# A sparse two-layer graph network on one core: ScalarE takes part of the list sorting, and the order around it changes

## The chip, the cores and the metric

The kernel runs on one core of a Trainium2 chip. The metric is the device time of one execution in microseconds; the median of three runs of the kernel before is 1572.41 us (1570.78 to 1575.34). Five engines work side by side, each through its own instructions in order: TensorE (PE; its weight loads are listed as PEld), VectorE (DVE), ScalarE (ACT), GpSimd (POOL) and SyncE (SP, which here only issues DMA transfers).

## What is computed

There are 16 graphs of 1024 nodes with 64 channels, and a dense weighted adjacency of 16 x 1024 x 1024, of which few entries are not zero. Two layers follow each other, each on the normed input and with a residual:

```
# layer 0: mean over the neighbours
h = relu(layernorm(x));  x = x + (adj / clip(adj.sum(2), 1)) @ h

# layer 1: per node a weighted quantile over its neighbours, then a small MLP
h = relu(layernorm(x))
nb = (adj > 0) without the diagonal;  m = nb.sum(-1)
skip = (m+1)//2 if m > 10 else 1               # every skip-th neighbour of a long list is removed,
removed = ...;  rem = removed | removed.T      # in both directions
vals = h[neighbours and self, not rem], sorted per channel
agg = 0.25*q(0.25) + 0.5*q(0.5) + 0.25*q(0.75) # each q interpolates between two sorted values
y = relu((h + agg) @ W1 + b1) @ W2 + b2;  x = x + y * mask
```

## The kernel before

**Layer 0.** The adjacency is read once, 128 rows at a time (tile `at`). ACT takes the sign of each row and its sum, DVE finds the numbers of the neighbours in it with Max8 (`listing`), PE turns it, and PE multiplies (`products`). `endings` sorts the nodes of a graph by the length of their list and scatters their records (channels, residual, list, number, mask) into a DRAM table `srt`, so that nodes of like length lie together. Four graphs make a group; there are four groups. `progress["batches"]` counts the graphs that are done.

**Lists.** `group(g)` reads the records of a group (`recs`, rows of 136 bytes), gathers one adjacency row for each node of the tile with the longest lists (`gat_rows`), works out from that which two neighbours are dropped and writes it into the DRAM table `tab`. It extracts the neighbours' numbers and makes jobs of them, one for each length class: ten in a group, for lists of 15 down to 1 places, with T nodes in each partition. `long_lists` does the like for the nodes with the longest lists, in four jobs of up to 88, 31, 24 and 20 places over all groups. There DVE searches the row for its numbers in many rounds of Max8 and MatchReplace (`lfound`, `lkeys`).

**A job** (`Job.run`, `sort`, `layers`): POOL gathers one place for each list entry by indirect DMA (64 channels and two numbers for each of 128 partitions) into A, named `places` or, for a long list, `lplaces`. DVE compares the two numbers with its own node number (`rem`, `gone`), counts what is valid and starts the weights (`wu`, finished by two ACT instructions). One wide DVE instruction adds 1e30 to the dropped places. Then DVE runs a sorting network of min and max instructions between A and a second copy (`other` in PSUM, or `long_other` in SBUF). The sorted places are multiplied by their weights, into `prod` for a short job and in place for a long one; `copies` says in which of the two copies (0 is A) each sorted place ended. PE adds the products up through the identity matrix (`pt`), ACT copies the sum out (`ot`), PE and ACT run the MLP (`ph`, `hid`, `py`, the first and last in `ps_small` banks). DVE adds the residual (`y`), and POOL scatters the finished rows to the output.

**The order.** The order of DVE and POOL instructions is written out in full by a planner at build time (`Plan`, lines 218 to 321). All parts are streams: a `yield` names an engine and a function that says when the next step can start. The planner keeps a clock for each engine, books a duration for each instruction (`note`), and always takes the stream that can start first; between equals the lower rank goes first. The durations are only a model: for ACT 0.06 us, 0.86 ns an element and 0.11 for each operand that is a pointer. `at(tile)` is when the tile is ready by the model, `room(name, n)` when a buffer of n comes free. Slack is added where the model must not be trusted: SLACK is 2 us, LOOSE 7. `later` puts the sorting of a job far back unless fewer than AHEAD = 16 gathers are open. On the chip nothing is reordered: if an instruction waits, all behind it on its engine wait.

Of the kernel before, what the change touches and what calls it, by code (L numbers as in the profile page):

```python
# [9 lines left out]
F32 = mybir.dt.float32  # L10
BF = mybir.dt.bfloat16
# [4 lines left out]
OP = mybir.AluOpType  # L16
# [195 lines left out]
AHEAD = 16  # L212
SLACK = 2.0
LOOSE = 7.0


class Timed:
# [13 lines left out]
class Plan:  # L231
# [24 lines left out]
    def room(self, name, bufs):  # L256

        tiles = self.slots.get(name, ())
        if len(tiles) < bufs:
            return 0.0  # L260
        old = tiles[-bufs]
        return INF if self.users[old] else max(self.used.get(old, 0.0), self.ready.get(old, 0.0))

    def at(self, *tiles):
        return max(self.ready.get(t.tensor.name, INF) for t in tiles)

    def note(self, engine, op, args, kwargs):
        if self.own is not None:
            self.clock[engine] = max(self.clock[engine], self.own)
        out = kwargs["out"] if "out" in kwargs else args[0]  # L270
        rest = [*args[0 if "out" in kwargs else 1:], *(v for k, v in kwargs.items() if k != "out")]
        rest = [getattr(v, "ap", v) if type(v).__name__.startswith("Indirect") else v for v in rest]
        rest = [v for v in rest if isinstance(v, bass.AP)]
        size = max(math.prod(v.shape[1:]) for v in (out, *rest[:2]))
        start = max(
            self.clock[engine],
            *(self.ready.get(v.tensor.name, 0.0) for v in rest if self.own is None),
            self.used.get(out.tensor.name, 0.0) if self.own is None else 0.0,
        )
        after = 0.15  # L280
        if engine == "DVE":
            half = op == "tensor_tensor" and all(v.dtype == HF for v in (out, *rest))
            time = 0.04 if op == "memset" else 0.07 + size * (0.57e-3 if half else 1.04e-3)
        elif engine == "ACT":
            pointers = sum(isinstance(kwargs.get(k), bass.AP) for k in ("bias", "scale"))
            time = 0.06 + size * 0.86e-3 + 0.11 * pointers + 0.09 * ("accum_out" in kwargs)
        elif engine == "PE":
            time = 0.1 + math.prod(out.shape[1:]) * 0.88e-3
            if op == "matmul" and rest[0].dtype == F32:
                time *= 2  # L290
        elif engine == "POOL":
            time, after = (1.27, 2.2) if op == "indirect_dma_start" else (0.15, 0.1)
            self.last = None
        else:
            start = max(start, self.clock["DMA"])
            time, after = 0.05, 2.2 + math.prod(out.shape) * 4 / 165e3
            self.clock["DMA"] = start + after - 2.2
        self.clock[engine] = end = start + time
        self.ready[out.tensor.name] = end + after
        for v in rest:  # L300
            self.used[v.tensor.name] = max(self.used.get(v.tensor.name, 0.0), end + after)
        if "accum_out" in kwargs:
            self.ready[kwargs["accum_out"].tensor.name] = end + after
        return start
# [59 lines left out]
def list_path(ctx, tc, x, adj, nodemask, w1, b1, w2, b2, out, go):  # L364
# [434 lines left out]
    class Job:  # L799
# [8 lines left out]
        def run(self):  # L808
            n, T, pool, short = self.n, self.T, self.pool, self.short

            since = []
            own = () if short else (lambda rank: self.rank,)
            pace = lambda: since[0] + 1.3 * len(since) if not short else 0.0
            yield "POOL", lambda: max(
                at(self.idx), room(self.name, self.bufs), room("S", 4) if short else 0.0
            ), *own
            A = self.A = new(pool, [P, n, T, W], F32, self.name, self.bufs, users=1)
            progress["ahead"] += T * (n - 1)
            if short:
                mine = self.S  # L820
                self.S = new(pool, [P, T, C], F32, "S", 4, users=1)
                nc.sync.dma_start(self.S, mine[:, :, :C])
                self.residual = mine[:, :, X1:R0]
            for t in range(T):
                for k in range(n - 1):
                    if t or k:
                        yield "POOL", pace, *own
                    since.append(since[0] if since else plan.clock["POOL"])
                    gather(A[:, k + 1, t, :], self.table, self.idx[:, t, k:k + 1])
                    progress["ahead"] -= 1  # L830
            yield "DVE", lambda: max(
                at(A, self.S) + SLACK, room("prod", 2) if short else 0.0,
                room("other" if short else "long_other", 1),
            ), self.later
            yield from self.sort()

        def later(self, rank):

            return rank - 900 if progress["ahead"] < AHEAD else rank + 2000

        def urgent(self):
            return -1000 if progress["ahead"] < AHEAD else 5000

        def sort(self):
# [5 lines left out]
                rem, A[:, 1:, :, C:],  # L850
                self.node.unsqueeze(1).unsqueeze(3).to_broadcast([P, n - 1, T, 2]), OP.is_equal,
            )
            gone = new(pool, [P, n - 1, T], F32, name + "gone", bufs)
            nc.vector.tensor_tensor(gone, rem[:, :, :, 0], rem[:, :, :, 1], OP.max)
            ok = new(pool, [P, n - 1, T], F32, name + "ok", bufs)
            nc.vector.scalar_tensor_tensor(
# [10 lines left out]
                q, taus.unsqueeze(2).to_broadcast([P, K, T]),  # L867
                valid.unsqueeze(1).to_broadcast([P, K, T]), OP.mult,
            )
            u = new(pool, [P, K, count, T], F32, name + "wu", 1)  # L870
            nc.vector.tensor_tensor(
                u, col_f[:, :count].unsqueeze(1).unsqueeze(3).to_broadcast([P, K, count, T]),
                q.unsqueeze(2).to_broadcast([P, K, count, T]), OP.subtract,
            )
            vals = A[:, 1:, :, :].rearrange("p k t w -> p (k t) w")[:, :, :C]
            nc.vector.scalar_tensor_tensor(
                vals,
                gone.rearrange("p k t -> p (k t)").unsqueeze(2).to_broadcast([P, (n - 1) * T, C]),
                HUGE, vals, op0=OP.mult, op1=OP.add,
            )  # L880
            if short:
                Bt = new(ps_o, [P, 3 * HALF], F32, "other", 1, users=1)
                other = Bt[:, :n * T * C].rearrange("p (k t c) -> p k t c", k=n, t=T)
            else:
                other = Bt = new(pool, [P, n, T, C], F32, "long_other", 1, users=1)
            yield "ACT", lambda: at(u) + SLACK
            nc.scalar.activation(u, u, AF.Abs)
            nc.scalar.activation(u, u, AF.Relu, bias=wt0, scale=-QUANTILES[0][1])

            def places(copy, run, shift=0):  # L890
                first, d1, n1, d2, n2 = run
# [36 lines left out]
            w = new(pool, [P, count, T], F32, name + "w", bufs)  # L928
            nc.vector.tensor_tensor(w, u[:, 0, :, :], u[:, 1, :, :], OP.add)
            nc.vector.scalar_tensor_tensor(w, u[:, 2, :, :], 2.0, w, op0=OP.mult, op1=OP.add)  # L930

            total = max(count + 1, 4)
            prod = None
            if short:
                prod = new(pool, [P, T, total, C], F32, "prod", 2, users=1)
                if count + 1 < total:
                    nc.vector.memset(prod[:, :, count + 1:, :], 0.0)
            for copy in range(2):
                for run in runs_of([k for k in range(count) if copies[k] == copy]):
                    first, step, number = run[:3]  # L940
                    sl = slice(first, first + step * (number - 1) + 1, step)
                    src = places(copy, run)
                    nc.vector.tensor_tensor(
                        prod[:, :, sl, :].rearrange("p t k c -> p k t c") if short else src, src,
                        w[:, sl, :].unsqueeze(3).to_broadcast([P, number, T, C]), OP.mult,
                    )
            if short:
                free(A)
                free(Bt)
                yield "ACT", lambda: at(S)  # L950
                nc.scalar.copy(prod[:, :, count, :], S[:, :, :C])
                free(S)

# [11 lines left out]
        def layers(self, terms, sources):  # L965

            T, R = self.T, terms[0][0].shape[1]
            yield "PE", lambda: max(at(*sources) + LOOSE, room("y", 5), room("pt", 2))
            y = new(mlp, [P, T, CO], F32, "y", 5, users=1)
            x1 = y  # L970
            if self.short:
                nc.sync.dma_start(x1, self.residual)
# [2 lines left out]
            for t0 in range(0, T, 4):  # L975
# [32 lines left out]
                for i, t in enumerate(ts):  # L1008
# [1 line left out]
                        pv[:, i, :], hid[:, i * P:(i + 1) * P], w2_sb, start=False,  # L1010
                        stop=(i == len(ts) - 1),
                    )
                yield "DVE", lambda: at(py) + LOOSE
                for i, t in enumerate(ts):
                    nc.vector.scalar_tensor_tensor(
                        y[:, t, :], pv[:, i, :], self.mask[:, t:t + 1], x1[:, t, :],
# [2 lines left out]
                free(py)  # L1019

            for t in range(T):
                yield "POOL", lambda: at(y) + LOOSE
                scatter(out_rows, y[:, t, :], self.nodes_i[:, t:t + 1], scatters)
            free(y)
            progress["jobs"][self.g] += 1
# [1 line left out]
    def group(g):  # L1027
# [17 lines left out]
        )  # L1045
        nodes_i = new(grp, [P, NTAU], I32, "nodes_i", 2)
        nc.vector.tensor_copy(nodes_i, nodes)
        yield "POOL", lambda: at(nodes_i)
        full = new(grp, [P, N], F32, "gat_rows", 1)
        gather(full, adj_rows, nodes_i[:, 0:1])  # L1050
        yield "DVE", always

        found = new(grp, [P, NTAU, 8 * NSEG], BF, "gfound", 1)
        nc.vector.tensor_scalar(found, lists, 0.0, None, op0=OP.is_gt)
        m = tiny.tile([P, NTAU], F32, name="gm")
        nc.vector.tensor_reduce(m, found, AX.X, OP.add)
# [52 lines left out]
        nc.vector.scalar_tensor_tensor(  # L1109
            full, col_f, node[:, 0:1], full, op0=OP.not_equal, op1=OP.mult  # L1110
        )
        nb = new(grp, [P, N], BF, "nb", 1)
        nc.vector.tensor_scalar(nb, full, 0.0, None, op0=OP.is_gt)
        cum = full
        nc.vector.tensor_tensor_scan(cum, nb, zeros, 0.0, op0=OP.add, op1=OP.add)
# [29 lines left out]
    def long_lists(pool):  # L1145
# [4 lines left out]
        for l, K in enumerate(LONG):  # L1150
# [7 lines left out]
                )  # L1158
            node = S[:, 0, RW - 2:RW - 1]
            mask = S[:, 0, RW - 1:RW]  # L1160
            yield "DVE", lambda: at(S)
            nodes = tiny.tile([P, 1], F32, name="lnodes")
            nc.vector.tensor_tensor(nodes, node, noff[:, 1:2], OP.add)
            nodes_i = new(pool, [P, 1], I32, "lnodes_i", 4)
# [62 lines left out]
            )  # L1227
            plan.add(job.run(), 100 * NG + l)

    progress = {"batches": 0, "groups": 0, "ahead": 0, "jobs": [0] * (NG + 1)}  # L1230
    for g in range(NG):
        plan.add(group(g), -2000)
    with tc.tile_pool(name="lay0", bufs=2) as pool:
# [303 lines left out]
```

## Time and profile before

| stretch, us | DVE busy | ACT busy | POOL busy | PE busy | granted clock |
|---|---|---|---|---|---|
| 0 to 845 (layer 0, first two groups) | 690.6 | 533.5 | 481.4 | 553.6 | 0.79 |
| 845 to 1572 (the rest of the lists) | 569.8 | 45.0 | 507.9 | 190.8 | 0.56 |

The span of the profiled execution is 1571.9 us, with 14933 instructions. DVE is busy for 1260.4 us of it, POOL for 989.3, PE for 744.4 and ACT for 578.5. In the second stretch POOL issues 399 gathers and 71 scatters of output rows.

How to read it: busy time is the union of an engine's instructions; the time from the end of one to the start of the next is idle time, put down to what released the next one ("issue" where nothing was waited for). A line of a group gives the engine, the operation, the names out<-in, how often, the busy time in us, the mean length of one in ns, and behind the second bar the idle time before them. All instructions have the line of the recording helper, L225, so groups are told apart by their tile names. A line of waits gives the sum in us, the number of times and the longest. In a timeline the first numbers are the start and the length in us.

### The profile page before, as it was taken

Reading aid. Unit: us, or ns where it says so; the run is one execution under the profiler, and the core shown is the slowest. Engines: PE = TensorE matmul, PEld = TensorE weight load, DVE = VectorE, ACT = ScalarE, POOL = GpSimd, SP = SyncE. Lnnn points to the kernel's source line nnn. Section 1 sums busy time; section 2 is a strip of 40 time slices with the busy share of each in tenths; the row PEclk is TensorE's granted clock in tenths of the full one; section 3 lists DMA queues with packets and bytes.
Section 4 is the critical chain, followed back from the end, with each engine's and each line's share of the span. In section 5 each row is a group of like instructions: output and inputs, shape, how many; then the busy total and the mean of one; then the engine's idle time right before and its main releaser. Section 6 shows DMA issues by size and latency. Waiting matters only on the chain. (4 is left out here: it accounts for less than half of the span.)

```text
span 1571.9 us, 14933 instructions
## 1 busy us (share of the span) xinstructions
PE 744.4 (47%) x3192; PEld 465.3 (30%) x3192; DVE 1260.4 (80%) x4174; ACT 578.5 (37%) x1746; POOL 989.3 (63%) x1149
## 2 busy tenths in 40 slices
PE   5787776365756754855880001200021367124355
PEld 2334443133343532532450001100021156023244
DVE  6767899997997699999556897659779889878962
ACT  7889888346565536664630000000000010000001
POOL 0222238665578767568676666587777678566775
PEclk8888998686977866976895555555555567555657
DMA  5455666244542433652222111111121111111110
GB/s 161 134 149 167 175 198 188 71 124 100 177 121 60 120 106 108 165 149 66 75 51 66 41 38 36 33 27 23 25 41 34 24 28 24 28 31 36 31 29 21
DMA packets 135530, 128.95 MB, mean 82 GB/s; under 512 B 100696, under 2 KB 103384, under 8 KB 135432
## 3 DMA queue, kind: packets, MB, share of 16 engines
q1 hardware_dynamic: 102696, 86.46, 19.7%
q0 software_dynamic: 32736, 41.47, 11.6%
q8 instruction: 27, 0.44, 0.1%
q14 instruction: 71, 0.58, 0.1%
HBM read 108.57 MB, written 19.28 MB: 81 GB/s over the span
## 5 line engine op out<-in xcount | busy, mean ns | idle before, releaser
L225 POOL DMA_INDIRECT places<-tab,idx x496 | 507.4, 1023 | 159.9 <-issue 146.1
L225 PE MATMUL pt<-ident,prod 128*128 128x128 f32 (+1 forms) x736 | 168.0, 395 | 627.5 <-DVE prod L225 586.7
L225 PEld LDWEIGHTS pt<-ident,prod 128*128 128x128 f32 (+1 forms) x736 | 136.6, 273 | 659.6 <-DVE prod L225 406.0
L225 PE MATMUL ps_small<-att,h 128*65 128x512 f32 x512 | 260.1, 657 | 44.1 <-ACT h L225 28.3
L225 POOL DMA_INDIRECT srt<-row,to x128 | 129.5, 1012 | 176.2 <-ACT row L225 154.8
L225 POOL DMA_INDIRECT lplaces<-tab,lidx x163 | 173.7, 1066 | 51.0 <-issue 47.9
L225 PE MATMUL pt<-ident,at 128*128 128x128 f32 x1024 | 167.3, 308 | 80.7 <-ACT att L225 68.9
L225 POOL DMA_INDIRECT out_dram<-y,nodes_i x124 | 130.6, 1053 | 99.2 <-DVE y L225 53.6
L225 DVE MAX8 rec<-sg 128x8 f16<-128x256 f16 x512 | 180.1, 414 | 4.4
L225 PEld LDWEIGHTS pt<-ident,at 128*128 128x128 f32 x1024 | 129.4, 157 | 126.2 <-ACT att L225 93.7
L225 ACT ACTIVATE sg<-at 128x1024 f16<-128x1024 f32 x128 | 134.9, 1054 | 54.2 <-DMA at<-in_adj_dram 34.6
L225 ACT COPY att<-pt 128x512 f32<-128x512 f32 x256 | 141.5, 582 | 22.7 <-PE pt L225 20.7
L225 ACT COPY ot<-pt 128x128 f32<-128x128 f32 (+3 forms) x56 | 22.2, 401 | 308.9 <-PE pt L225 308.6
L225 ACT ACTIVATE wu<-wu 128x39 f32<-128x39 f32 (+9 forms) x40 | 9.4, 235 | 337.7 <-DVE wu L225 337.6
L225 PEld LDWEIGHTS ps_small<-att,h 128*65 128x65 f32 x512 | 75.8, 154 | 184.3 <-issue 128.5
L225 DVE TENSOR_TENSOR sg<-sg,keyed 128x1024 f16<-128x1024 f16 x128 | 87.6, 684 | 37.3 <-ACT sg L225 37.2
L225 DVE SCALAR_TENSOR_TENSOR y<-ps_small,recs,y 128x64 f32<-128x64 f32 x124 | 28.0, 276 | 81.0 <-PE ps_small L225 80.9
L225 DVE TENSOR_TENSOR other<-places,other 128x64 f32<-128x64 f32 (+6 forms) x204 | 69.7, 342 | 5.6
L225 DVE TENSOR_TENSOR places<-places,other 128x64 f32<-128x64 f32 (+2 forms) x208 | 62.4, 309 | 4.9
L225 DVE TENSOR_TENSOR long_other<-lplaces 128x512 f32<-128x512 f32 (+5 forms) x124 | 63.9, 553 | 0.4
L225 DVE TENSOR_TENSOR lplaces<-long_other 128x512 f32<-128x512 f32 (+7 forms) x116 | 61.4, 567 | 0.1
L225 DVE TENSOR_TENSOR places<-other,places 128x128 f32<-128x128 f32 (+5 forms) x160 | 54.9, 343 | 3.5
(206 smaller groups left out, 1516.1 us busy)
## 6 DMA issues: line engine op xcount, KB each, us to landing
at<-in_adj_dram SPq DMA_DIRECT2D x128, 512.0 KB
places<-tab,idx POOLq DMA_INDIRECT x496
tab<-row SPq DMA_DIRECT2D x16, 264.0 KB
xt<-in_x_dram SPq DMA_DIRECT2D x16, 256.0 KB
lplaces<-tab,lidx POOLq DMA_INDIRECT x163
recs<-srt SPq DMA_DIRECT2D x4, 544.0 KB
srt<-row,to POOLq DMA_INDIRECT x128
out_dram<-y,nodes_i POOLq DMA_INDIRECT x124
```

The source lines that it names most:

```text
L225: ins = getattr(self._engine, op)(*args, **kwargs)
```

## The change

After layer 0 is done (`helped`), ACT takes two parts of the sorting from DVE: the 1e30 for dropped places, one Identity with a bias for each place and node, and the multiplication with the weights, one scaled copy for each: of copy 0 for short jobs and of all places for long ones. The preparation of a job becomes a step of its own before the sort (`soon`), so that ACT can work in between; `gone` and `wu` get buffers for two short jobs. Besides, the search of long lists waits until the last group's records have been begun (`begun`); DMA loads of rows under 512 bytes are booked at a lower rate; the last addition and the scatter of a job are put later in the order (LATE instead of LOOSE); there are six `y` buffers, and two row tiles of a group (`gfound`, `nb`) share one buffer.

```diff
+LATE = 14.0
...
-            time, after = 0.05, 2.2 + math.prod(out.shape) * 4 / 165e3
+            rate = 165e3 if 4 * out.shape[-1] >= 512 else 85e3
+            time, after = 0.05, 2.2 + math.prod(out.shape) * 4 / rate
...
             yield "DVE", lambda: max(
-                at(A, self.S) + SLACK, room("prod", 2) if short else 0.0,
-                room("other" if short else "long_other", 1),
-            ), self.later
+                at(A, self.S) + SLACK,
+                *(room(("" if short else "l") + name, 2 if short else 1) for name in ("gone", "wu")),
+            ), self.soon
             yield from self.sort()
...
+        def soon(self, rank):
+
+            return rank - (950 if progress["ahead"] < AHEAD else -1900)
...
-            gone = new(pool, [P, n - 1, T], F32, name + "gone", bufs)
+            gone = new(pool, [P, n - 1, T], F32, name + "gone", bufs, users=1)
...
-            u = new(pool, [P, K, count, T], F32, name + "wu", 1)
+            u = new(pool, [P, K, count, T], F32, name + "wu", bufs, users=1)
...
-            vals = A[:, 1:, :, :].rearrange("p k t w -> p (k t) w")[:, :, :C]
-            nc.vector.scalar_tensor_tensor(
-                vals,
-                gone.rearrange("p k t -> p (k t)").unsqueeze(2).to_broadcast([P, (n - 1) * T, C]),
-                HUGE, vals, op0=OP.mult, op1=OP.add,
-            )
+
+            helped = progress["batches"] == B
+            if helped:
+                yield "ACT", lambda: at(gone) + SLACK
+                nc.scalar.mul(gone, gone, HUGE)
+                for t in range(T):
+                    for k in range(1, n):
+                        if (t or k > 1) and k % 4 == 1:
+                            yield "ACT", always
+                        val = A[:, k, t, :C]
+                        nc.scalar.activation(val, val, AF.Identity, bias=gone[:, k - 1, t:t + 1])
+            else:
+                vals = A[:, 1:, :, :].rearrange("p k t w -> p (k t) w")[:, :, :C]
+                nc.vector.scalar_tensor_tensor(
...
+            free(gone)
+            yield "ACT", lambda: at(u) + SLACK
+            nc.scalar.activation(u, u, AF.Abs)
+            nc.scalar.activation(u, u, AF.Relu, bias=wt0, scale=-QUANTILES[0][1])
+            yield "DVE", lambda: max(
+                at(A) + SLACK if helped else 0.0, room("prod", 2) if short else 0.0,
+                room("other" if short else "long_other", 1),
+            ), self.later
...
-            yield "ACT", lambda: at(u) + SLACK
-            nc.scalar.activation(u, u, AF.Abs)
-            nc.scalar.activation(u, u, AF.Relu, bias=wt0, scale=-QUANTILES[0][1])
...
+            free(u)
...
-            for copy in range(2):
-                for run in runs_of([k for k in range(count) if copies[k] == copy]):
+
+            helped = progress["batches"] == B
+            for copy in (1, 0):
+                mine = [k for k in range(count) if copies[k] == copy]
+                if helped and (copy == 0 or not short):
+                    yield "ACT", lambda: at(w) + SLACK
+                    for e, k in enumerate(mine):
+                        if e and e % 4 == 0:
+                            yield "ACT", always
+                        for t in range(T):
+                            src = places(copy, (k, 1, 1, 1, 1))[:, 0, t, :]
+                            nc.scalar.activation(
+                                prod[:, t, k, :] if short else src, src, AF.Copy,
+                                scale=w[:, k, t:t + 1],
+                            )
+                    continue
+                for run in runs_of(mine):
...
-                yield "ACT", lambda: at(S)
+                if not helped:
+                    yield "ACT", lambda: at(S)
...
-            yield "PE", lambda: max(at(*sources) + LOOSE, room("y", 5), room("pt", 2))
-            y = new(mlp, [P, T, CO], F32, "y", 5, users=1)
+            yield "PE", lambda: max(at(*sources) + LOOSE, room("y", 6), room("pt", 2))
+            y = new(mlp, [P, T, CO], F32, "y", 6, users=1)
...
-                yield "DVE", lambda: at(py) + LOOSE
+                yield "DVE", lambda: at(py) + LATE
...
-                yield "POOL", lambda: at(y) + LOOSE
+                yield "POOL", lambda: at(y) + LATE
...
         nc.vector.tensor_copy(nodes_i, nodes)
+        progress["begun"] = g + 1
...
-        found = new(grp, [P, NTAU, 8 * NSEG], BF, "gfound", 1)
+        found = new(grp, [P, N], BF, "gfound", 1).rearrange("p (t e) -> p t e", t=NTAU)
...
-        nb = new(grp, [P, N], BF, "nb", 1)
+        nb = new(grp, [P, N], BF, "gfound", 1)
...
-            yield "DVE", lambda: at(S)
+            yield "DVE", lambda: at(S) + SLACK if progress["begun"] == NG else INF
...
-    progress = {"batches": 0, "groups": 0, "ahead": 0, "jobs": [0] * (NG + 1)}
+    progress = {"batches": 0, "begun": 0, "groups": 0, "ahead": 0, "jobs": [0] * (NG + 1)}
```

More of the change, by code (lines that the diff above doesn't have):

```diff
@@ L874, in sort @@
             )
-            vals = A[:, 1:, :, :].rearrange("p k t w -> p (k t) w")[:, :, :C]
-            nc.vector.scalar_tensor_tensor(
-                vals,
-                gone.rearrange("p k t -> p (k t)").unsqueeze(2).to_broadcast([P, (n - 1) * T, C]),
-                HUGE, vals, op0=OP.mult, op1=OP.add,
-            )
+            helped = progress["batches"] == B
[11 more added lines that the diff above has]
+                nc.vector.scalar_tensor_tensor(
+                    vals,
+                    gone.rearrange("p k t -> p (k t)").unsqueeze(2).to_broadcast(
+                        [P, (n - 1) * T, C]
+                    ),
+                    HUGE, vals, op0=OP.mult, op1=OP.add,
+                )
[7 more added lines that the diff above has]
+            ), self.later
             if short:
@@ L937, in sort @@
                     nc.vector.memset(prod[:, :, count + 1:, :], 0.0)
-            for copy in range(2):
-                for run in runs_of([k for k in range(count) if copies[k] == copy]):
+            helped = progress["batches"] == B
[11 more added lines that the diff above has]
+                                scale=w[:, k, t:t + 1],
+                            )
+                    continue
+                for run in runs_of(mine):
                     first, step, number = run[:3]
```

## The prediction

> **What bounds the kernel now.** I read first the share of each engine by stretches, then the costliest groups and the waits after layer 0, then the timelines around single waits. By stretch (columns: PE, PEld, DVE, ACT, POOL busy us, then the granted clock, DMA share, GB/s):
> ```profile
> 0.00:845.00 845.00, 553.55 (x2308) 316.07 (x2308) 690.58 (x2333) 533.54 (x1619) 481.43 (x621) 0.79 0.46 126
> 845.00:1572.00 727.00, 190.84 (x884) 149.23 (x884) 569.82 (x1842) 44.98 (x127) 507.92 (x529) 0.56 0.15 30
> ```
> Two stages. Layer 0 and the first lists end at about 845 us; there VectorE (DVE) is busy 82% and ScalarE (ACT) 63%. In the last 727 us ACT is nearly free (45 us), so work given to it there has room. DVE (570) and GpSimd (POOL, 508) share the load. POOL's number understates it: between two indirect DMAs lies an issue gap of 0.30.
> ```profile
> L225 POOL DMA_INDIRECT places<-tab,idx x236 | 245.2, 1039 | 74.0 <-issue 70.5 <-DMA places<-tab,idx 2.1 <-DMA tab<-drop,didx 1.4
> L225 POOL DMA_INDIRECT lplaces<-tab,lidx x163 | 173.7, 1066 | 51.0 <-issue 47.9 <-PE pt L225 1.6 <-DMA lplaces<-tab,lidx 1.5
> L225 POOL DMA_INDIRECT out_dram<-y,nodes_i x67 | 72.3, 1080 | 57.5 <-DVE y L225 41.1 <-issue 7.3 <-DVE lrem L225 5.4
> ```
> An undisturbed gather starts every 1.25 us (median 0.947 busy + 0.30). POOL runs from 850 to 1564, 714 us. I went through its timeline and added all idle time above 0.3: 72 us. So POOL has about 642 us of work that nothing hides, of which some 49 is stretching: gathers over 0.96 us. DVE has 570 us of work and 120 us of waits. POOL is the tighter engine and the order of both is fixed in the program, so each makes the other wait. The waits:
> ```profile
> DVE y L225 <- PE ps_small L225: 74.1, 16, 9.4
> DVE lrem L225 <- DMA lplaces<-tab,lidx: 21.7, 1, 21.7
> DVE rem L225 <- DMA places<-tab,idx: 14.0, 1, 14.0
> POOL out_dram L225 <- DVE y L225: 41.1, 11, 10.8
> POOL gat_rows L225 <- DVE lkeys L225: 9.9, 1, 9.9
> ```
> DVE reaches the last addition of a job (y) 4.6 us too early on average, since TensorE (PE), at half clock here, has not finished; POOL's scatter then waits behind it. The other DVE waits, lrem and rem, are for gathers: the sign that POOL limits. How a wide DVE instruction stretches a gather (start, length):
> ```profile
> 1041.13 6.02 DVE L225 SCALAR_TENSOR_TENSOR lplaces<-lgone,lplaces 128x5632 f32<-128x5632 f32 x1
> 1041.24 0.37 ACT L225 ACTIVATE lwu<-lwu 128x201 f32<-128x201 f32 x1 [24.68 <-DVE lwu L225]
> 1041.65 0.47 ACT L225 ACTIVATE lwu<-lwu,wt 128x201 f32<-128x201 f32 x1
> 1041.84 6.12 POOL L225 DMA_INDIRECT lplaces<-tab,lidx  x1 [0.30 <-issue]
> ```
> The gather that meets the marking of dropped places takes 6.12 instead of 0.95. A scatter beside the product of 4.56 us at 1299.4 takes 4.47.
>
> **What the Trainium skill says.** (1) "ScalarE: Activation LUTs", section "What ACT_TABLE_LOAD costs": an ACTIVATE with a per-partition pointer as bias takes about 280 ns + 0.833 per element, a second pointer about 93 more, and back-to-back ones overlap by about 93. For 64 elements: 333 alone, 240 in a row. The trace agrees: the squares of layer 0 (one pointer, 64 elements) take 333, and eight Relus with two pointers take 2.76 us together, 0.33 each. (2) "SBUF — State Buffer", section "Who interferes with whom": a DVE instruction with two SBUF inputs holds a port against GpSimd's reads, and it infers that descriptor generation is not hit by it. On this second point the trace differs, by the 6.12 above; I go by the trace. (3) "Perfetto Trace Analysis", section "GPSIMD Engine Instruction": GpSimd spans are unreliable, the spacing of starts is to be used; hence the 1.25 and the waits from the timeline above.
>
> **The change, part by part.**
> *Dropped places to ACT.* After layer 0, 20 short jobs and 4 long ones are sorted. DVE's marking leaves: from the groups by shape 19.6 us short (2 each of 1.50, 1.35, 1.22, 1.15, 1.09, 0.95, 0.82, 0.68, 0.55, 0.48) and 11.5 long (6.0+2.2+1.8+1.5). ACT gets one 64-wide Identity per gathered place: 2x124 + 163 = 411, at 0.24 (page 1) 99 us.
> *Weights to ACT.* The products of copy 0 of short jobs leave DVE, 10.9 us, and all of the long ones, 9.7: lplaces 8.9 and long_other 0.7. ACT gets 122 + 127 = 249 scaled copies, 60 us. Its load becomes 45+160 = 205 of 727: hidden. DVE keeps about 570-52 = 518.
> *What ACT now holds up.* DVE's sorting waits for the marks. For the 88 places of the longest list that is 21 us (6.0 before), for a short job 1.2 to 4.8 (0.5 to 1.5 before). The planner books 0.06+0.055+0.11 = 0.225 for one, near the 0.24, and puts other DVE work between; at 5% to 7% off, 88 of them are 1.3 us late, inside the 2 us slack. Behind ACT's in-order queue stand also the copies that wait for PE (ot, hid). A late PE now delays marks, and so DVE. Bounds: nothing, or for all 24 jobs what DVE waits per y today, 4.6 each, 110 us. I take 25 us of new DVE waits, as the ot copies are planned with slack of their own, and DVE has 120 us of idle time to lose first.
> *POOL freed from wide DVE work.* The two large pieces stretch POOL by 5.2 and 3.5. The remaining 52-10.6 = 41 us of removed DVE work I charge at the mean rate of the other DVE instructions on two SBUF inputs (about 40 us of stretch over 254 long network + 41): 0.14, 6 us. Together 15. Bounds: 9 and 25.
> *LATE and six y buffers.* The addition and the scatter come 7 us later each in the two orders. All DVE y waits but one (9.42) are under 7 us, and the scatters have 14 us: of POOL's 41 (and the 5.4 and 5.4 behind lrem and other) I let 10 stay. Gain on POOL about 35 to 40; I take 30, as some are replaced by other waits, bounds 10 and 42. The sixth y pays for the longer holding; a ps_small bank is held 7 us longer, which matters only in layer 0.
> *Key search after the last group.* Today the search of the longest list (838 to 865) and the beginning of the last group interleave, and POOL waits 9.9 for the group's row number. The search now comes after it. The last group begins when the jobs of the second are done, which LATE puts up to 14 us later in the order; but POOL has some 110 gathers of the third group left, and DVE idles about 20 us around 816 to 838, in which a job of that group can be prepared. The long gathers may start 10 to 20 us later (897.9 now): POOL does short ones meanwhile. I take 7 of the 9.9 as gain; bounds -8 and +10.
> *Packet times, soon, shared gfound, order of copies.* Loads with rows under 512 B are booked at 85 instead of 165 KB per us. The records need 8.6 us from issue to first use (186.2 to 194.8): booked 5.6 before, 8.8 now. Better order, no work of its own: 0. Preparing a job before its sort spends no more DVE time, and gfound is read long before nb is written: 0. Layer 0 loses no DVE work; its order moves, which I bound at +-8 and take at 0.
> Sum: 15+30+7 = 52 on POOL's chain, less 4 for the new ACT waits that reach POOL (25 of DVE, mostly into its idle time): 48. 1572-48 = **1524 us**.
>
> **The rivals.**
> *A, half the waits return.* ACT stands behind a late PE and DVE stops at the marks rather than at y. POOL gets 15 and a third of the 37: 27 us, 1545. For: ACT's idle column today is all PE and DVE. Against: the marks' own slack.
> *B, slower.* The 110 us of new DVE waits come in full, the idle 120 is already spent waiting for gathers, and each short job keeps its places 8 us longer (marks and products on ACT), with four buffers: POOL waits 4 us for a buffer in each of 24 jobs, 96 in place of the 72, and gains 15 at most from stretching; 1572+24-15 = 1581, with the later long list (8) 1589. For: with the search later and marks of 21 us the longest list, 155 us of sorting, starts later. Against: DVE has only 518 us of work in 714.
> *C, POOL alone.* If nearly all waits go and stretching falls by 25, POOL ends 90 us earlier: about 1485. Against: the drain after the last gather (1538 to 1564) is mostly scatters, which must be done anyway.
>
> **How the numbers follow.** Forecast 0.52, A 0.27, B 0.13, C 0.05, no change 0.03. The range leaves C and most of B out: 1490 to 1570, which also covers the bounds of the single costs (9+10-8 = 11 to 25+42+10 = 77) but for layer 0. Faster by over 0.3%: 0.82; within 0.3%: 0.04; slower: 0.14.
>
> **What would show it.** After the last layer 0 record: DVE busy near 518 and ACT near 205; no marking group on DVE but ACT Identity groups at about 0.33 alone and 0.24 in a row; y waiting for ps_small well under 30 us; POOL idle above the issue gap near 30 instead of 72; no gather of 4 to 6 us; the row gather of the last group not waiting for lkeys; layer 0's end within 8 us of 845. It is wrong if DVE waits for places written by ACT in tens of us, if POOL waits for buffers, if the last group begins so late that POOL runs dry, or if layer 0 ends later, where ps_small is shared with its products.

## The result, and the profile after

The changed kernel takes 1526.41 us (median of four runs, 1525.97 to 1526.61), the kernel before 1571.6 beside it: a ratio of 0.971, interval 0.969 to 0.973. A later run gave 1525.06 against 1571.07. By stretches (columns as before: PE, PEld, DVE, ACT, POOL busy us, then clock, DMA share, GB/s):

```profile
0.00:845.00 845.00, 552.73 (x2278) 316.42 (x2278) 679.16 (x2305) 547.18 (x1689) 464.52 (x603) 0.78 0.46 125
845.00:1524.00 679.00, 198.76 (x914) 152.83 (x914) 532.76 (x1815) 205.76 (x816) 496.27 (x554) 0.57 0.18 35
```

In the second stretch ACT went from 45 to 206 us and DVE from 570 to 533, though 25 more POOL instructions lie in it: the boundary at 845 us no longer cuts the work at the same place. The groups of gathers and scatters in this stretch, and then the ACT instructions that took over the work (whole run):

```profile
L226 POOL DMA_INDIRECT places<-tab,idx x231 | 233.6, 1011 | 71.5 <-issue 65.2 <-DMA places<-tab,idx 3.7 <-DMA tab<-drop,didx 1.4
L226 POOL DMA_INDIRECT lplaces<-tab,lidx x163 | 166.9, 1024 | 53.7 <-issue 49.1 <-PE pt L226 4.3 <-DMA lplaces<-tab,lidx 0.3
L226 POOL DMA_INDIRECT out_dram<-y,nodes_i x79 | 77.2, 977 | 26.3 <-issue 13.1 <-DVE y L226 10.8 <-DVE places L226 0.6
```
```profile
L226 ACT ACTIVATE places<-places,gone 128x64 f32<-128x64 f32 x283 | 70.7, 335 | 0.4
L226 ACT ACTIVATE lplaces<-lplaces,lgone 128x64 f32<-128x64 f32 x163 | 40.0, 338 | 0.1
L226 ACT ACTIVATE prod<-places,w 128x64 f32<-128x64 f32 x157 | 39.5, 335 | 63.1 <-DVE w L226 63.1
L226 ACT ACTIVATE lplaces<-lplaces,lw 128x64 f32<-128x64 f32 x124 | 31.0, 337 | 18.3 <-DVE lw L226 18.3
```

The scatters' waits for y fell from 41.1 to 10.8. The mean gather and scatter is shorter by 28 to 103 ns. One ACT instruction lasts 0.335 us, but 163 of them fill only 40.0: 0.245 each in a row. What DVE waits for now in the second stretch, and below it POOL:

```profile
DVE lrem L226 <- DMA lplaces<-tab,lidx: 29.2, 1, 29.2
DVE y L226 <- PE ps_small L226: 23.8, 6, 9.2
DVE long_other L226 <- ACT lplaces L226: 21.6, 7, 4.7
DVE other L226 <- ACT places L226: 16.7, 4, 6.5
```
```profile
POOL lat L226 <- DVE lnodes_i L226: 16.8, 3, 8.0
POOL out_dram L226 <- DVE y L226: 10.8, 3, 5.4
POOL lplaces L226 <- PE pt L226: 4.3, 1, 4.3
POOL gat_rows L226 <- DVE lnodes_i L226: 1.8, 1, 1.8
```

DVE's waits for y went from 74.1 to 23.8; in their place stand waits for ACT, 40 us in this stretch. The marks (the 1e30 added to dropped places) of the longest list show how they look: 88 in one row of 21.10 us, and the first network instructions of DVE following them, each as soon as its places are marked.

```profile
1088.84 21.10 ACT L226 ACTIVATE lplaces<-lplaces,lgone 128x64 f32<-128x64 f32 x88
1089.04 0.37 DVE L226 TENSOR_TENSOR lwu<-col_f,lq 128x201 f32<-128x201 f32 x1
...
1093.03 0.69 DVE L226 TENSOR_TENSOR long_other<-lplaces 128x512 f32<-128x512 f32 x1 [3.62 <-ACT lplaces L226]
1096.85 0.69 DVE L226 TENSOR_TENSOR long_other<-lplaces 128x512 f32<-128x512 f32 x1 [3.12 <-ACT lplaces L226]
```

**An account of POOL.** From POOL's timeline I take for each run three numbers: the end of its last scatter; the sum of the idle times over 0.45 us before its indirect DMAs, less 0.3 each ("waits"); and what its 931 indirect DMAs take over 0.96 us ("stretch"). The device time is the end and some 8 to 12 us.

| kernel | time, us | ratio, interval | end | waits | stretch | end less both |
|---|---|---|---|---|---|---|
| before | 1570 to 1574 | 1 | 1564 | 312 | 75 | 1176 |
| changed | 1525 | 0.972 (0.969 to 0.974) | 1515 | 293 | 48 | 1174 |
| LATE alone, on before | 1551 | 0.988 (0.985 to 0.991) | 1540 | 289 | 76 | 1175 |
| changed, ACT takes nothing | 1560 | 0.991 (0.989 to 0.993) | 1552 | 304 | 72 | 1176 |
| changed, LATE off | 1526 | 0.970 (0.968 to 0.972) | 1517 | 293 | 48 | 1176 |
| ACT's part alone, with the separate preparation | 1546 | 0.984 (0.982 to 0.987) | 1536 | 309 | 52 | 1175 |
| ACT takes nothing, VectorE in pieces | 1548 | 0.985 (0.983 to 0.988) | 1540 | 310 | 55 | 1175 |

What is left after waits and stretch is 1174 to 1176 us in every kernel. This is bookkeeping: POOL issues the same DMAs in all of them, so every change of its end must appear in the two middle columns, and each edit can be read by what it does to them. That the rest is constant does not show which engine bounds. VectorE passes the same test: its end less its idle times over 0.45 us is 1325 to 1330 us in the four kernels in which it does the marks, and 1279 to 1282 in the others.

What speaks for POOL is something else. After the last record scatter of layer 0 it waits for 73 of 738 us in the kernel before and for 36 of 725 in the changed one, while DVE idles for 132 of 732 and 152 of 717. And two edits below (LATE alone, and VectorE in pieces) shorten the time while DVE's work stays or grows. Ahead of that scatter POOL waits for 237 to 262 us in every kernel; in the kernel before, 155 us of this are for the records that ACT writes (`row`). There POOL does not bound.

The kernel before itself took 1570.4 to 1574.0 us beside these runs, so a difference between two rows is good to about 4 us.

### The profile page after: what moved, and what is told of

Its sections match the earlier page's. It is cut to its first block, busy times and chain, and to the rows that moved or that the text cites. A ratio compares the mean times of both kernels' runs of the same rounds, so it can differ in the third digit from the quotient of the medians.

```text
span 1523.8 us, 15747 instructions
## 1 busy us (share of the span) xinstructions
PE 751.5 (49%) x3192; PEld 469.3 (31%) x3192; DVE 1211.9 (80%) x4119; ACT 752.9 (49%) x2503; POOL 960.8 (63%) x1156
## 3 DMA queue, kind: packets, MB, share of 16 engines
q0 software_dynamic: 32736, 41.47, 12.6%
## 5 line engine op out<-in xcount | busy, mean ns | idle before, releaser
L226 POOL DMA_INDIRECT places<-tab,idx x496 | 495.0, 998 | 161.2 <-issue 142.3
L226 PE MATMUL pt<-ident,prod 128*128 128x128 f32 (+1 forms) x736 | 159.1, 376 | 454.0 <-DVE prod L226 369.6
L226 PEld LDWEIGHTS pt<-ident,prod 128*128 128x128 f32 (+1 forms) x736 | 129.4, 257 | 486.1 <-ACT prod L226 287.8
L226 PE MATMUL pt<-ident,at 128*128 128x128 f32 x1024 | 181.0, 324 | 106.7 <-ACT att L226 79.2
L226 POOL DMA_INDIRECT lplaces<-tab,lidx x163 | 166.9, 1024 | 53.7 <-issue 49.1
L226 PEld LDWEIGHTS pt<-ident,at 128*128 128x128 f32 x1024 | 138.5, 166 | 154.2 <-ACT att L226 104.8
L226 POOL DMA_INDIRECT out_dram<-y,nodes_i x124 | 121.8, 983 | 37.9 <-issue 20.0
L226 PE MATMUL ps_small<-ot,w_sb 128*128 128x128 f32 (+3 forms) x112 | 53.1, 564 | 53.3 <-ACT ot L226 22.5
L226 ACT ACTIVATE places<-places,gone 128x64 f32<-128x64 f32 x283 | 70.7, 335 | 0.4
L226 ACT ACTIVATE prod<-places,w 128x64 f32<-128x64 f32 x157 | 39.5, 335 | 63.1 <-DVE w L226 63.1
```

The costliest lines, as they stand in the source:

```text
L226: ins = getattr(self._engine, op)(*args, **kwargs)
```

## Experiments

**1. The parts taken out one at a time, on two chips that issue slowly.** Marks and weights back on DVE (e1, again as f1), LATE and the sixth y buffer off (e2, f2), key search free (e3), packet times off (e4):

```diff
# e1, f1 (in two places)
-            helped = progress["batches"] == B
+            helped = False
# e2, f2
-LATE = 14.0
+LATE = 7.0
# (and y with 5 buffers)
# e3
-            yield "DVE", lambda: at(S) + SLACK if progress["begun"] == NG else INF
+            yield "DVE", lambda: at(S)
# e4
-            rate = 165e3 if 4 * out.shape[-1] >= 512 else 85e3
+            rate = 165e3
```

> The changed kernel with the marks and the weights back on VectorE (ScalarE takes nothing); all else as changed. Theory (GpSimd's order bounds the list stage): only the freed stretching is lost, 15 us, and VectorE's 52 us more fit mostly into its idle time: 1540 to 1550. Rival 1 (VectorE bounds): nearly the whole 52 us come back: 1570 to 1580. Rival 2 (the gain is a lucky order, any small edit moves it): anywhere from 1520 to 1575, and gathers stretched no more than in the changed kernel.

> The changed kernel with LATE at 7 us as LOOSE was, and five y buffers. Theory: the waits of the scatters for y return, about 30 us on GpSimd: 1550 to 1560, with more than 25 us of GpSimd waits for y. Rival 1 (VectorE bounds): VectorE waits for ps_small return, 50 us or more, but hide in the ScalarE offload: 1530 to 1540. Rival 2 (lucky order): unforeseeable, waits for y no guide to the time.

> The changed kernel with the key search of long lists free to start as soon as its rows are read. Theory: 7 us of GpSimd waiting around the last group's beginning return: 1530 to 1536. Rival 2 (lucky order): no relation, plus or minus 20.

> The changed kernel with all loads booked at 165 KB per us again. Theory: no work of its own, the time stays within 5 us of 1526, unless it is this edit that ended layer 0 35 us earlier (last record scatter at 790.8 instead of 826.2); then that scatter is back near 826. Rival 2 (lucky order): 1515 to 1550 with a different order.

> The same kernel as in the first call (the changed kernel with marks and weights back on VectorE), on a chip where the kernel before takes its usual 1572 us. Theory (GpSimd's order bounds the list stage): 15 us of stretching and a little of VectorE's 52 us come back: 1540 to 1550, and gathers of 4 to 6 us return. Rival 1 (VectorE bounds): 1570 to 1580. Rival 2 (lucky order): 1520 to 1575 with no relation to the stretching. If ScalarE again issues one instruction in 0.7 to 1.4 us, the chip decides, and the run says nothing on the theories.

> The same kernel as in the first call (the changed kernel with LATE at 7 us and five y buffers), on a chip where the kernel before takes its usual 1572 us. Theory: GpSimd's waits for y come back by 25 us or more: 1550 to 1560. Rival 1 (VectorE bounds): 1530 to 1540. Rival 2 (lucky order): waits for y no guide to the time.

On these two chips the kernel before itself took 1924 and 1906 us, so the times don't compare with those above. Measured, as ratios to before: e1 1.027 (1.023 to 1.030), f1 1.024 (1.018 to 1.030), e2 1.044 (1.041 to 1.048), f2 1.036 (1.032 to 1.040), e3 1.058 (1.055 to 1.061), e4 1.051 (1.047 to 1.054). What the traces show of it is late issue. In e3 some marks of the longest list start 1.40 us apart instead of 0.24, with a length of 0.35 as ever:

```profile
1389.39 0.35 ACT L226 ACTIVATE lplaces<-lplaces,lgone 128x64 f32<-128x64 f32 x1 [1.05 <-issue]
1390.79 0.35 ACT L226 ACTIVATE lplaces<-lplaces,lgone 128x64 f32<-128x64 f32 x1 [1.05 <-issue]
1392.19 0.35 ACT L226 ACTIVATE lplaces<-lplaces,lgone 128x64 f32<-128x64 f32 x1 [1.05 <-issue]
```

It is not ACT alone: in these six traces 47 to 70 instructions of PE and 40 to 62 of DVE follow an idle time of over 0.35 us put down to issue; before and after have at most 2. Why the issue is late is not shown.

The times decide nothing on the theories. Three things hold in these traces all the same. POOL's end less waits and stretch is again 1174 to 1175, at ends of 1942 to 2029. The stretch is less than with usual issue, but again larger with marks on DVE (53 and 55) than with marks on ACT (24 to 35), and only e1 and f1 have a gather over 5 us. And the order shows which edit moved layer 0: after its last record scatter stand 236 short gathers in the kernel before, 268 in the changed kernel, in e1, f1 and e3, but 237 in e2 and f2 and 244 in e4. So it takes both LATE and the packet times to put 32 gathers behind layer 0, while taking out ScalarE's part or the later search changes nothing in this. The effects do not add up, though: with LATE and the packet times both off (i1 below) it is 249, with LATE alone (g2 below) 245.

**2. The changed kernel again, and LATE alone on the kernel before** (with the sixth y buffer, and the shared row tile for space):

```diff
-                yield "DVE", lambda: at(py) + LOOSE
+                yield "DVE", lambda: at(py) + LATE
...
-                yield "POOL", lambda: at(y) + LOOSE
+                yield "POOL", lambda: at(y) + LATE
```

> The changed kernel itself, unaltered, on the chip of the experiments. If the chip takes its usual 1572 us for the kernel before: 1526 us, ratio 0.971. If instructions are issued as slowly as in the first six runs (before 1906 to 1924 us): theory says the ScalarE part then costs more than it brings, because some 640 more ScalarE instructions of 0.7 us and more pass through one queue, so the changed kernel is slower than before, ratio 1.02 to 1.06, and slower than with ScalarE's part taken out (1.024 to 1.027). Rival: the ratio 0.97 holds on any chip, so that LATE off (1.036 to 1.044) and the others cost 7 points and more.

> The kernel before with LATE = 14 us for the last addition and the scatter, six y buffers and the shared group row tile (for the space); nothing on ScalarE, search and rates as before. Theory: this alone takes out most of GpSimd's waits for y, ratio 0.975 to 0.985 where before takes 1572 us (1533 to 1549); the gather of 6 us beside the wide marking stays. Rival 1 (VectorE bounds, the offload is the gain): 0.995 to 1.0. Rival 2 (lucky order): 0.97 to 1.01 with no relation to the waits for y.

Both ran on a chip with usual issue: 1525.06 and 1551.18 us. LATE alone takes 20 us, all of it waits (312 to 289), and leaves the stretch at 76; it falls just short of the 0.975 to 0.985 that I gave it. After layer 0 the scatters' waits for y fall from 41.1 to 12.6, while the wait for the last group's row grows from 9.9 to 17.5. Rival 1's 0.995 is excluded. Whether the changed kernel is slower than before on a slow chip stays open: it was not run on one.

**3. ACT off and LATE off on chips with usual issue**, the kernels of e1 and e2:

> The changed kernel with marks and weights back on VectorE, third attempt, for a chip where the kernel before takes its usual 1571 us. Theory (GpSimd's order bounds the list stage): the stretching that the six slow runs showed as well (40 us of it in the list stage with VectorE marking, 15 to 17 with ScalarE) comes back in part, and a little of VectorE's 52 us: 1540 to 1550. Rival 1 (VectorE bounds): as LATE alone gave 20 us, all of the other 26 and more: 1550 to 1575. Rival 2 (lucky order): below 1530.

> The changed kernel with LATE at 7 us and five y buffers, third attempt, for a chip where the kernel before takes its usual 1571 us. Theory: LATE alone gave 20 us on the kernel before, so 20 to 30 go: 1545 to 1556, with 20 us and more of GpSimd waits for y back, and layer 0's last record scatter later than 791. Rival 1 (VectorE bounds): ScalarE's offload covers it, 1526 to 1538. Rival 2 (lucky order): over 1560 or below 1526.

Measured 1559.50 (1557.47 to 1561.78) and 1526.46 (1524.69 to 1526.90). Both go against my sizes and agree with the first rival's, though 1526.46 lies at the edge of the second's too. Without ACT's part 34 us come back (30 by the ratios), without LATE nothing. The account says through what. ACT off: stretch 48 to 72, all of it after layer 0, and waits 293 to 304, together 35. That the order is fixed shows here as well: e1 is this kernel, its POOL waited for 736 us instead of 304, and POOL's 1154 instructions come in the same order in both. The two long instructions are back, each beside a gather that it holds:

```profile
1077.74 6.02 DVE L226 SCALAR_TENSOR_TENSOR lplaces<-lgone,lplaces 128x5632 f32<-128x5632 f32 x1
...
1078.40 6.18 POOL L226 DMA_INDIRECT lplaces<-tab,lidx  x1 [0.30 <-issue]
...
1337.85 4.55 DVE L226 TENSOR_TENSOR lplaces<-lplaces,lw 128x4224 f32<-128x4224 f32 x1
1338.28 4.94 POOL L226 DMA_INDIRECT places<-tab,idx  x1 [0.31 <-issue]
```

LATE off: the sum of waits is the same 293 but lies elsewhere. After the last record scatter it is 50 instead of 34, before it 243 instead of 259. Of the 16 us, 8 are waits of scatters for y (16.9 instead of 9.0; I had expected 20 and more). So LATE still does what it is for in part, and what it wins in the list stage it gives back in layer 0, whose order it also changes.

**4. ACT's part alone, and VectorE in pieces.** i1 is the changed kernel with LATE, the later search and the packet times all undone; the preparation as a step of its own stays. i2 is e1 with marks and weights on DVE cut so that no instruction has more than 512 elements:

```diff
-                nc.vector.scalar_tensor_tensor(
-                    vals, gone..., HUGE, vals, op0=OP.mult, op1=OP.add)
+                for r in range(0, (n - 1) * T, 8):
+                    e = min(r + 8, (n - 1) * T)
+                    nc.vector.scalar_tensor_tensor(
+                        vals[:, r:e, :], flat[:, r:e]..., HUGE, vals[:, r:e, :], ...)
...
-                for run in runs_of(mine):
+                part = max(8 // T, 1)
+                for run in [
+                    (r[0] + r[1] * a, r[1], min(part, r[2] - a), 1, 1)
+                    for r in runs_of(mine) for a in range(0, r[2], part)
+                ]:
```

> The changed kernel without LATE (7 us, five y buffers), without the later key search and with all loads booked at 165 KB per us: what is left is ScalarE's part and the preparation as a step of its own. Revised theory (GpSimd's last instruction ends at 1175 us plus its waits plus its stretching; ScalarE's part takes 18 us of stretching and with it waits that LATE would also have taken): stretching near 48 in the whole run, waits 290 to 305, time 1521 to 1538. Rival (search or packet times carry the rest of the gain): 1540 to 1556. On a chip with slow issue: ratio over 1.02, no word on either.

> The kernel with marks and weights back on VectorE (1559.5 us), but in pieces of at most 512 elements instead of instructions of up to 5632: VectorE's load stays, and grows by some 7 us for the pieces. Theory that the width of the instructions holds GpSimd up: the 17 us of stretching that marks and weights cause fall to about 5 (the rate of the sorting network, 0.085 us for each us, on 51 us), no gather over 3 us, time 1546 to 1554. Rival, that VectorE's load itself is what ScalarE took away: 1559 to 1567.

i1: 1545.90 (ratio 0.984), in the range of the rival (search or packet times carry the rest of the gain). Stretch 52 is near the 48 expected; the waits are 309, above my 290 to 305 and only 3 below those of the kernel before. So the ACT part alone is worth 25 us, nearly all of it stretch. And the later search and the packet times bring some 20 more when LATE is off (h2 differs from i1 only by these two): the waits go from 309 to 293. Which of the two does it was not tried on a usual chip. Beside LATE and without ACT's part the same two, with the separate preparation, bring nothing (0.991 in h1 against 0.988 for LATE alone). So what these settings of the order do to the waits depends on what stands beside them, and a lucky order, my rival 2, is not excluded for this part of the gain.

i2: 1547.97 (0.985), as the theory of the width had it. With VectorE's load as large as in h1 and a little larger (1266 us busy, 1262 there), the time falls by 11.5 us (9 by the ratios). The stretch falls from 72 to 55. I put each stretched DMA after layer 0 down to the DVE instruction that covers it longest: marks and weights account for 19 us in h1 and for 5.5 in i2. The same marks are now eleven instructions; seven of them in one window, beside gathers of full speed:

```profile
1077.42 4.42 DVE L226 SCALAR_TENSOR_TENSOR lplaces<-lgone,lplaces 128x512 f32<-128x512 f32 x7
1078.02 0.94 POOL L226 DMA_INDIRECT lplaces<-tab,lidx  x1 [0.30 <-issue]
1079.27 0.94 POOL L226 DMA_INDIRECT lplaces<-tab,lidx  x1 [0.31 <-issue]
1080.52 0.94 POOL L226 DMA_INDIRECT lplaces<-tab,lidx  x1 [0.30 <-issue]
```

But two DMAs of over 3 us, which I had excluded, remain (3.12 and 3.37). They lie beside rows of short instructions of the sorting network, with no gap between them:

```profile
1483.22 3.37 POOL L226 DMA_INDIRECT places<-tab,idx  x1 [0.30 <-issue]
1483.48 0.56 DVE L226 TENSOR_TENSOR other<-places 128x384 f32<-128x384 f32 x1
...
1485.36 0.41 DVE L226 TENSOR_TENSOR long_other<-long_other,lplaces 128x256 f32<-128x256 f32 x1
1485.70 0.95 DVE L226 TENSOR_TENSOR other<-places,other 128x768 f32<-128x768 f32 x1
```

So short instructions alone do not free POOL in every case. Between i2 and the changed kernel 23 us are left: waits 310 to 293 and stretch 55 to 48. Whether this part is VectorE's load or the other order is not shown.

## Why the prediction was right, and where its steps were not

The forecast was 1524 and the time is 1526. The frame held: less stretch and fewer waits on POOL. That the number came so near is luck: the waits fell by 18 us where 33 were forecast, the stretch by 27 where 15 were, and the two misses cancelled.

- **What bounds**: POOL in the list stage, as said; it has the least waits there (73 us, DVE 132), and edits that only spare POOL shorten the time.
- **Waits of the list stage**: I let POOL's 72 fall by 37 (30 for LATE, 7 for the search). After the last record scatter they fell from 73 to 36. The size was right, the cause only in part. The wait for the last group's row went from 9.9 to 1.8, but POOL's waits for the long lists' rows (lat) rose from 10.0 to 16.8: most of the 7 was given back. And LATE is not needed for the whole: LATE off costs nothing, and there the later search and the packet times, which I took at 7 and 0, bring 19.
- **Layer 0**: a step that failed. I bounded it at 8 us and took 0. Its last record scatter came at 791 instead of 826 us, with 32 short gathers moved behind it, and POOL's waits before that scatter grew from 239 to 258. It is the term that took back 19 of the 37.
- **Stretch**: taken as 15, bounds 9 and 25; it fell by 27 over the whole run, 19 of it after the last record scatter. Put down to DVE instructions as above, marks and weights account for 20 of 49 in the kernel before: 7.5 and 5.1 for long and short marks, 5.0 and 2.1 for weights. The network accounts for some 24 before and after.
- **ScalarE's part as a whole**: the mis-sized term. I gave it the 15 of stretch less 4 for new waits, 11 us net; taking it out of the changed kernel costs 34, 24 of stretch and 10 of waits, and alone it brings 25, 23 of stretch and 3 of waits. So its stretch was taken too small in both. The 52 us that leave DVE I had charged at nothing beyond that, because DVE idles for 120. Alone that nearly holds. Beside the other edits 10 us of waits hang on it; that a DVE with less to do ends them would explain this, but it is not shown. Rival 1 of the experiments had the sizes, but DVE as the bound does not fit: LATE alone wins 20 us with DVE busy for 1262 us, as before.
- **New waits for ACT**: 48 us of DVE in the whole run (27 for places, 22 for lplaces) against 25 taken and a bound of 110. The pitch of 0.245 agrees with the 0.24 worked out from the Trainium skill's page "ScalarE: Activation LUTs", section "What ACT_TABLE_LOAD costs". ACT grew by 174 us instead of 160, since three more jobs fell behind layer 0; the run's DVE time fell by 48.5 instead of 52.
- **Sum**: waits 312 to 294 and stretch 75 to 48 in the profiled run, 46 of the 48 us by which POOL ends earlier. Predicted: waits 33 and stretch 15.

## What to carry to other kernels

Where a queue keeps its order and its work, split its end into waits, stretching and a rest: each edit can then be judged by the first two sums. The constant rest does not say that this queue is the bound; compare how long each engine waits in the stage, and change one without the other. A helper engine that takes work from a neighbour with idle time can still pay, by removing long instructions that hold up the bounding queue's DMAs; cutting such instructions into pieces brings a part of it with no offload at all. Edits to slack in a planned order are not additive: LATE won 20 us alone and nothing beside the others, so take such settings out again once the rest is in place.

## What the runs showed of the hardware

A long DVE instruction with two SBUF inputs holds up an indirect DMA of POOL that starts during it, nearly always to 0.8 to 0.9 us after its own end (6.02 us beside 6.18, 4.55 beside 4.94). The order of the two starts decides: in the eight traces with usual issue, of 156 DMAs that started 0.04 us or more after the marks, weights and row searches of over 1 us, 150 ended so; 63 that started up to 0.4 us before them, or by 0.03 us after, took 0.94 to 1.02. This goes against the inference on the Trainium skill's page "SBUF — State Buffer", section "Who interferes with whom", that descriptor generation is not hit. With one input in PSUM (`other`) it does not happen. In the kernel before:

```profile
1201.35 1.49 DVE L225 TENSOR_TENSOR prod<-other,w 128x1280 f32<-128x1280 f32 x1
1202.05 0.94 POOL L225 DMA_INDIRECT places<-tab,idx  x1 [0.30 <-issue]
...
1524.67 1.36 DVE L225 TENSOR_TENSOR prod<-places,w 128x1152 f32<-128x1152 f32 x1
1524.79 2.11 POOL L225 DMA_INDIRECT out_dram<-y,lnodes_i  x1 [0.30 <-DVE w L225]
```

In these eight traces 16 DMAs that started during the first of these forms took 0.95 us on average, 10 during the second 1.94 (all of them at least 0.7 us before its end). In the row of eleven marks of i2 the gathers start together with every second instruction and take 0.94 us each. A row of network instructions held one for 3.37 us, to 0.82 us after the last of them with two SBUF inputs; what decides between the two rows is not shown.

And in the runs on two chips ACT instructions of 0.35 us started 0.70 to 1.40 us apart in places, the kernel before took 21% to 22% more, and POOL's rest of 1174 us did not change. Whether the chip or the hour made this is not shown, as each was used once.
